# A graph layer on one core: gathered rows split into two float32r halves, h transposed kept in DRAM

## The chip, the cores and the metric

The kernel runs on one core of a Trainium2 chip. The core has five engines that work side by side and meet at semaphores: TensorE (PE, matrix products into PSUM), VectorE (DVE), ScalarE (ACT), GpSimd (POOL) and SyncE (SP). SP, ACT and POOL also issue DMA transfers, which 16 DMA engines of the core carry out between DRAM and the on-chip memory SBUF. The metric is the device time of one execution in microseconds.

## The reference, cut to what matters

```python
h = jnp.maximum(_layernorm(x, axis=-1), 0.0)          # x: 12500 x 256, float32
agg = jax.ops.segment_sum(h[src], dst, num_segments=N)  # 200000 edges, dst sorted
z = (1.0 + eps_gin) * h + agg
t = jnp.dot(z, W1) + b1                                # 256 -> 512
t = jax.nn.relu(_batchnorm(t, g1, bt1))                # statistics over all 12500 rows
conv_out = jnp.dot(t, W2) + b2                         # 512 -> 256
out = x + jax.nn.relu(_batchnorm(conv_out + h, g2, bt2))
```

`src` and `dst` have 200000 entries between 0 and 12499. For each edge the row `src` of h is added into row `dst` of the aggregate. `dst` comes sorted, so neighbouring edges have neighbouring targets. Everything is float32.

## The kernel before, in words

The rows are cut into 25 chunks of 512 (the last has 212). Four stages follow one another, all in `fast()`.

1. **Layernorm** (L274 to L294). A chunk of x is loaded with four consecutive rows in each partition. VectorE takes the statistics, ScalarE applies them with the ReLU (L259). The rows go to a table in DRAM, `h_tab`, from which they are gathered later. TensorE transposes the chunk (L285), and VectorE and ScalarE copy the result into `hT` (L292, L294), which stays in SBUF to the end: 25 tiles, features in partitions, nodes along the columns. Since four rows lie in a partition, the copy has a stride of four.

2. **Gather and first layer** (L297 to L420). The 200000 edges are cut into 1563 tiles of 128 edges (the last has 64), and these into 131 groups of 12 (`GT`). `gather(i)` has POOL issue one indirect DMA a tile (L328): it reads 128 indices from a column of `srcT` in SBUF and brings 128 rows of h, 1 KB each, into a group's buffer `gt`. The pool `gat` has `AHEAD + 1` = 3 such buffers; POOL is two groups ahead. `sums(i)` makes a one-hot matrix `oh` of each edge's target relative to the first target of its group (VectorE, L353) and has TensorE add up the group's rows by target: 12 products of `oh` with `gt` in one PSUM tile `ps` (L362). Products of float32 show as two passes in the trace, so a group has 24. The sums are copied to `zs` (ScalarE, L367); a second one-hot, `at` (VectorE, L369), says at which column of the result they belong. `put(i)` transposes and places them by two products (L380), and VectorE adds the result into the chunk's `zc` (L389), which ScalarE has filled with (1 + eps) h from `hT` (L342). As soon as no later group can reach a chunk, `first_layer` multiplies it by W1 (L397), takes statistics (L401), and stores t in `t_tab` in DRAM. The column numbers that both one-hots are compared with, `col`, are kept in PSUM.

3. **Second layer** (L425 to L446). Each chunk of t is loaded, normalized (ScalarE, L434), multiplied by W2 (L441), added to `hT` (L445), and its statistics are taken.

4. **Output** (L451 to L472). ScalarE normalizes `hT` (L460), TensorE transposes it back (L467), VectorE adds x (L471), and ACT's queue stores the rows.

The order of instructions on each engine comes from a scheduler that follows the program's order and moves instructions where its own estimate of times suggests it. Each engine, and each DMA queue that SP, ACT or POOL feeds, takes its instructions strictly in that order. Dependencies between engines become semaphore waits.

The lines that matter below: L328 (gathers, POOL), L353, L369 and L389 (VectorE in the gather stage), L362 (`ps`, TensorE), L342 and L367 (ScalarE), L285 to L294 (transposes and copies of h), L460 to L472 (output).

Of the kernel before, what the change touches and what calls it, by code (L numbers as in the profile page):

```python
# [7 lines left out]
F32 = mybir.dt.float32  # L8
I32 = mybir.dt.int32
AF = mybir.ActivationFunctionType  # L10
OP = mybir.AluOpType
# [3 lines left out]
P = 128  # L15
R = 4
EPS = 1e-5
GT = 12
MARGIN = 76
AHEAD = 2  # L20

# [7 lines left out]
def kernel(  # L29
# [16 lines left out]
    nc = tc.nc  # L46
    N, D = x.shape
# [214 lines left out]

    def fast():
        with ExitStack() as fs:
            keep = fs.enter_context(tc.tile_pool(name="keep", bufs=1))
            t_tab = dram.tile([NCH, P, HC, CH], F32, name="t_tab")

            hT = [keep.tile([P, DC, w * R], F32, name=f"hT{g}") for g, (_, w) in enumerate(chunks)]


            with tc.tile_pool(name="ln", bufs=3) as ln, tc.tile_pool(
                name="ps_h", bufs=2, space=PSUM
            ) as ps_h:
                for g in range(NCH):  # L274
                    n0, w = chunks[g]
                    n = w * R
                    xt = ln.tile([P, R, D], F32, name="xt", bufs=4)
                    move(nc.sync, xt, x, g, store=False)
                    ht = ln.tile([P, R, D], F32, name="ht")
                    layernorm(ln, xt, w, ht)  # L280
                    move(nc.sync, ht, h_tab, g, store=True)
                    pz = ps_h.tile([P, DC, CH], F32, name="pz")
                    for d in range(DC):
                        for c in range(R):
                            nc.tensor.transpose(  # L285
                                pz[:, d, c * w : (c + 1) * w], ht[:w, c, d * P : (d + 1) * P],
                                ident[:w, :w],
                            )
                        side = hT[g][:, d, :].rearrange("p (w c) -> p c w", c=R)
                        came = pz[:, d, :n].rearrange("p (c w) -> p c w", c=R)  # L290
                        if d % 2:
                            nc.scalar.copy(side, came)  # L292
                        else:
                            nc.vector.tensor_copy(side, came)  # L294


            with ExitStack() as es:  # L297
                gat = es.enter_context(tc.tile_pool(name="gat", bufs=AHEAD + 1))
                sel = es.enter_context(tc.tile_pool(name="sel", bufs=2))
                zcp = es.enter_context(tc.tile_pool(name="zc", bufs=3))  # L300
                tsp = es.enter_context(tc.tile_pool(name="ts", bufs=2))
# [20 lines left out]
                def gather(i):  # L322
                    t0, n = groups[i]
                    gs = []
                    ga = gat.tile([P, GT, D], F32, name="gt")
                    for t in reversed(range(t0, t0 + n)):
                        rows = left if t == full_tiles else P
                        nc.gpsimd.indirect_dma_start(  # L328
                            out=ga[:rows, t - t0, :], out_offset=None, in_=h_tab,
                            in_offset=bass.IndirectOffsetOnAxis(ap=srcT[:rows, t : t + 1], axis=0),  # L330
                        )
                        gs.append((t - t0, rows))
                    gathered[i] = ga, gs

                zc = {}

                def z_chunk(c):
                    if c in zc or c >= NCH:
                        return
                    n = chunks[c][1] * R  # L340
                    zc[c] = zcp.tile([P, DC, CH], F32, name="zc")
                    nc.scalar.activation(zc[c][:, :, :n], hT[c], AF.Copy, scale=gin1)  # L342

                def span(i):
                    return STEP * i - MARGIN, STEP * i - MARGIN + WIDE

                summed = {}

                def sums(i):

                    t0, n = groups[i]
                    oh = sel.tile([P, GT, P], F32, name="oh")
                    nc.vector.tensor_tensor(  # L353
                        oh[:, :n, :],
                        col[:, :P].unsqueeze(1).to_broadcast([P, n, P]),
                        dstT[:, t0 : t0 + n].unsqueeze(2).to_broadcast([P, n, P]),
                        op=OP.is_equal,
                    )
                    ga, gs = gathered.pop(i)
                    ps = ps_s.tile([P, D], F32, name="ps")  # L360
                    for k, (j, rows) in enumerate(gs):
                        nc.tensor.matmul(  # L362
                            ps, lhsT=oh[:rows, j, :], rhs=ga[:rows, j, :], start=(k == 0),
                            stop=(k == n - 1),
                        )
                    zs = sel.tile([P, D], F32, name="zs", bufs=3)
                    nc.scalar.copy(zs, ps)  # L367
                    at = sel.tile([P, WIDE], F32, name="at")
                    nc.vector.tensor_scalar(  # L369
                        at, col, shift[:, i : i + 1], None, op0=OP.is_equal  # L370
                    )
                    summed[i] = zs, at

                def put(i):

                    lo, hi = span(i)
                    zs, at = summed.pop(i)
                    pz = ps_z.tile([P, DC, CH], F32, name="pz2")
                    for d in range(DC):
                        nc.tensor.matmul(  # L380
                            pz[:, d, :WIDE], lhsT=zs[:, d * P : (d + 1) * P], rhs=at, start=True, stop=True
                        )
                    for c in range(max(lo, 0) // CH, -(-min(hi, N) // CH)):
                        z_chunk(c)
                        a, b = max(lo, c * CH, 0), min(hi, (c + 1) * CH, N)
                        if a >= b:
                            continue
                        side = zc[c][:, :, a - c * CH : b - c * CH]
                        nc.vector.tensor_add(side, pz[:, :, a - lo : b - lo], side)  # L389

                def first_layer(c):
# [13 lines left out]

                done = 0
                for i in range(min(AHEAD, NG)):
                    gather(i)
                for i in range(NG + 1):
                    if i + AHEAD < NG:  # L410
                        gather(i + AHEAD)
                    if i < NG:
                        sums(i)
                    if i == 0:
                        continue
                    put(i - 1)
                    nxt = span(i)[0] if i < NG else N
# [5 lines left out]


            with tc.tile_pool(name="tin", bufs=4) as tin, tc.tile_pool(name="tsb", bufs=2) as tsb, tc.tile_pool(  # L425
                name="ps_y", bufs=4, space=PSUM
            ) as ps_y:
                for g in range(NCH):
                    n = chunks[g][1] * R
                    ti = tin.tile([P, HC, CH], F32, name="ti")  # L430
                    nc.sync.dma_start(ti[:, :, :n], t_tab[g, :, :, :n])
                    tT = tsb.tile([P, HC, CH], F32, name="tT")
                    for f in range(HC):
# [4 lines left out]
                    for d in range(DC):  # L438
                        py = ps_y.tile([P, CH], F32, name="py")
                        for f in range(HC):  # L440
# [3 lines left out]
                            )  # L444
                        nc.vector.tensor_add(hT[g][:, d, :], py[:, :n], hT[g][:, d, :])  # L445
                        nc.vector.bn_stats(st2[:, d, g, :], hT[g][:, d, :])  # L446

            sc2, of2 = norm(keep, st2, mv2, DC, g2c, bt2c, b2c, "2")


            with tc.tile_pool(name="xin", bufs=6) as xin, tc.tile_pool(name="ysb", bufs=3) as ysb, tc.tile_pool(  # L451
                name="ps_o", bufs=3, space=PSUM
            ) as ps_o:
                for g in range(NCH):
                    n0, w = chunks[g]
                    xt = xin.tile([P, R, D], F32, name="xr")
                    move(nc.sync, xt, x, g, store=False)
                    yr = ysb.tile([P, DC, R, P], F32, name="yr")
                    for d in range(DC):
                        nc.scalar.activation(  # L460
                            yr[:, d, :, :w], hT[g][:, d, :].rearrange("p (w c) -> p c w", c=R),
                            AF.Relu, bias=of2[:, d : d + 1], scale=sc2[:, d : d + 1],
                        )
                    po = ps_o.tile([P, R, D], F32, name="po")
                    for c in range(R):
                        for d in range(DC):
                            nc.tensor.transpose(  # L467
                                po[:w, c, d * P : (d + 1) * P], yr[:, d, c, :w], ident
                            )
                    ot = ysb.tile([P, R, D], F32, name="ot")  # L470
                    nc.vector.tensor_add(ot[:w], po[:w], xt[:w])  # L471
                    move(nc.scalar, ot, out, g, store=True)  # L472

# [250 lines left out]
```

## Time and profile before

| | us |
|---|---|
| median of 3 runs (lowest, highest) | 2654.84 (2652.75, 2655.27) |
| the profiled execution's own time | 2652.91 |
| its span, first to last instruction | 2651.0 |
| layernorm, up to the start of the first gather | to 149.1 |
| gathers, start of the first to end of the last | 149.1 to 2362.2 |
| second layer, first to last product with W2 | 2392 to 2558.5 |
| output stage | 2558.5 to 2651 |

| from 149 to 2362 us | busy us of 2213 |
|---|---|
| POOL | 1481.5 |
| TensorE, passes | 1314.4 |
| VectorE | 431.2 |
| ScalarE | 123.7 |
| DMA engines (share) | 0.34 |

How to read the lines. A line of the group view names the source line, engine, operation, output and inputs with their shapes, and how many there were; behind the first bar stand the busy time in us and the mean of one in ns; behind the second the idle time of the engine just before these instructions, and what ended it. "issue" is time in which the engine waited for nothing that the profile shows. "remote" is a semaphore whose sender the profile does not show. The view of waits gives engine, line, what was waited for, the total in us, how often, and the longest. In the timeline a line has its start, its duration, and in brackets the idle time before it. PE stands for passes of TensorE, PEld for its weight loads.

### The profile page before, as it was taken

The numbers are of one execution on the slowest core, as the hardware profiler recorded it, in microseconds if no ns is written. First come the engines' busy times: TensorE is split into PE (matmuls) and PEld (weight loads), VectorE is DVE, ScalarE is ACT, GpSimd is POOL, SyncE is SP. The second block draws the span as 40 slices with busy tenths as digits, with TensorE's granted clock in tenths as the row PEclk, the third lists the DMA queues.
The fourth block names the chain that finished last, engine by engine and source line by source line (L and its number), as shares of the span: only waits on it lengthen the run. The fifth ranks groups of instructions, "written<-read, shape, count | busy, mean of one in ns | idle before, by whom it ended". The sixth has DMA issues, their size and how long they took to land.

```text
span 2651.0 us, 14241 instructions
## 1 busy us (share of the span) xinstructions
PE 1623.6 (61%) x4881; PEld 1029.4 (39%) x4881; DVE 633.8 (24%) x1017; ACT 346.8 (13%) x561; POOL 1483.4 (56%) x1575
## 2 busy tenths in 40 slices
PE   3564556755665576556456556666565656569985
PEld 2333344433443343334334334434343334444444
DVE  6611121211221122112112112121121212124443
ACT  4710000000000000000000000000000000004446
POOL 0056667666766666666676676666666676640000
PEclk6566677776776786767777766767776677779985
DMA  5633333333333333333333333333333333325437
GB/s 176 227 101 90 95 101 115 105 95 101 115 105 95 111 105 105 96 111 105 107 97 109 106 98 102 110 105 112 95 105 110 91 114 102 111 78 214 159 130 281
DMA packets 101342, 310.96 MB, mean 117 GB/s; under 512 B 27684, under 2 KB 32362, under 8 KB 95118
## 3 DMA queue, kind: packets, MB, share of 16 engines
q0 software_dynamic: 75008, 204.90, 26.3%
q1 hardware_dynamic: 21744, 91.21, 9.6%
q10 hardware_dynamic: 4510, 13.86, 1.3%
q8 instruction: 41, 0.67, 0.1%
q14 instruction: 39, 0.32, 0.0%
HBM read 258.66 MB, written 51.20 MB: 117 GB/s over the span
## 4 chain that ended last, share of the span: by engine, by line
issue 28%; PE 26%; POOL 25%; another core or an unknown queue 9%; DMA 3%; DVE 2%; ACT 2%; ACTq 0%; POOLq 0%
POOL gt L328 25%; PE ps L362 13%; PE py L441 6%; PE ph L397 4%; DMA gt<-h_tab,srcT 3%; PE pz L380 2%; ACT yr L460 2%; DVE oh L353 1%; PE po L467 1%; DVE zc L389 1%; DVE ot L471 0%; DVE mv L229 0%; DVE at L369 0%; DVE st L401 0%
## 5 line engine op out<-in xcount | busy, mean ns | idle before, releaser
L328 POOL DMA_INDIRECT gt<-h_tab,srcT x1563 | 1481.8, 948 | 850.5 <-issue 458.2
L362 PE MATMUL ps<-gt,oh 128*128 128x256 f32 x3126 | 987.1, 447 | 643.0 <-issue 559.4
L362 PEld LDWEIGHTS ps<-gt,oh 128*128 128x128 f32 x3126 | 672.5, 221 | 949.5 <-issue 738.8
L389 DVE TENSOR_TENSOR zc<-pz,zc 128x560 f32<-128x560 f32 (+9 forms) x203 | 101.0, 527 | 1518.0 <-PE ps L362 863.5
L380 PE MATMUL pz<-at,zs 128*128 128x280 f32 x524 | 194.5, 498 | 181.4 <-DVE zc L389 114.8
L367 ACT COPY zs<-ps 128x256 f32<-128x256 f32 x131 | 48.9, 373 | 1739.4 <-PE ps L362 1147.3
L397 PE MATMUL ph<-zc,w1s 128*128 128x512 f32 (+1 forms) x400 | 197.0, 648 | 80.4 <-DVE zc L389 56.9
L353 DVE TENSOR_TENSOR oh<-col,dstT 128x1536 f32<-128x1536 f32 x131 | 227.8, 1739 | 14.5 <-issue 14.5
L380 PEld LDWEIGHTS pz<-at,zs 128*128 128x128 f32 x524 | 119.5, 237 | 235.0 <-issue 209.2
L441 PE MATMUL py<-tT,w2s 128*128 128x512 f32 (+1 forms) x400 | 169.5, 587 | 4.6 <-ACT tT L434 4.6
L397 PEld LDWEIGHTS ph<-zc,w1s 128*128 128x128 f32 x400 | 82.4, 211 | 181.1 <-issue 117.5
L401 DVE BATCH_NORM_STATS2 st<-ph 128x6 f32<-128x512 f32 (+1 forms) x100 | 68.4, 684 | 265.9 <-remote 93.7
L441 PEld LDWEIGHTS py<-tT,w2s 128*128 128x128 f32 x400 | 76.4, 192 | 97.7 <-issue 86.7
L402 ACT COPY ts<-ph 128x512 f32<-128x512 f32 (+1 forms) x100 | 57.3, 573 | 334.0 <-DVE st L401 251.9
L285 PE MATMUL pz<-ident,ht 128*128 128x128 f32 (+1 forms) x200 | 65.0, 442 | 54.1 <-ACT ht L259 19.5
L434 ACT ACTIVATE tT<-ti,of,sc 128x512 f32<-128x512 f32 (+1 forms) x100 | 72.3, 796 | 91.3 <-issue 86.4
L467 PE MATMUL po<-ident,yr 128*128 128x128 f32 (+1 forms) x200 | 47.6, 413 | 35.6 <-ACT yr L460 35.6
L285 PEld LDWEIGHTS pz<-ident,ht 128*128 128x128 f32 (+1 forms) x200 | 36.6, 205 | 82.5 <-ACT ht L259 40.7
L369 DVE TENSOR_SCALAR at<-col,shift 128x280 f32<-128x280 f32 x131 | 65.5, 500 | 0.0
L460 ACT ACTIVATE yr<-hT,of,sc 128x512 f32<-128x512 f32 (+1 forms) x50 | 59.9, 1276 | 20.1 <-DVE ot L471 19.2
L445 DVE TENSOR_TENSOR hT<-py,hT 128x512 f32<-128x512 f32 (+1 forms) x50 | 33.9, 678 | 100.9 <-PE py L441 100.9
L467 PEld LDWEIGHTS po<-ident,yr 128*128 128x128 f32 (+1 forms) x200 | 37.5, 214 | 45.7 <-ACT yr L460 45.7
(68 smaller groups left out, 307.6 us busy)
## 6 DMA issues: line engine op xcount, KB each, us to landing
gt<-h_tab,srcT POOLq DMA_INDIRECT x1563
t_tab<-ts SPq DMA_DIRECT2D x24, 1024.0 KB
ti<-t_tab SPq DMA_DIRECT2D x24, 1024.0 KB
xt<-in_x_dram SPq DMA_DIRECT2D x24, 512.0 KB
h_tab<-ht SPq DMA_DIRECT2D x24, 512.0 KB
xr<-in_x_dram SPq DMA_DIRECT2D x24, 512.0 KB
out_dram<-ot ACTq DMA_DIRECT2D x24, 512.0 KB
rawi_d<-in_dst_dram SPq DMA_DIRECT2D x1, 768.0 KB
```

The lines of the kernel that those rows point to most:

```text
L285: nc.tensor.transpose(pz[:, d, c * w : (c + 1) * w], ht[:w, c, d * P : (d + 1) * P], ident[:w, :w],)
L328: nc.gpsimd.indirect_dma_start(out=ga[:rows, t - t0, :], out_offset=None, in_=h_tab, in_offset=bass.IndirectOffsetOnAxis(ap=srcT[:rows, t ...
L353: nc.vector.tensor_tensor(oh[:, :n, :], col[:, :P].unsqueeze(1).to_broadcast([P, n, P]), dstT[:, t0 : t0 + n].unsqueeze(2).to_broadcast([P ...
L362: nc.tensor.matmul(ps, lhsT=oh[:rows, j, :], rhs=ga[:rows, j, :], start=(k == 0), stop=(k == n - 1),)
L380: nc.tensor.matmul(pz[:, d, :WIDE], lhsT=zs[:, d * P : (d + 1) * P], rhs=at, start=True, stop=True)
L389: nc.vector.tensor_add(side, pz[:, :, a - lo : b - lo], side)
L397: nc.tensor.matmul(ph[:, :n], lhsT=w1s[:, d, f * P : (f + 1) * P], rhs=zc[c][:, d, :n], start=(d == 0), stop=(d == DC - 1),)
L401: nc.vector.bn_stats(st1[:, f, c, :], ph[:, :n])
L434: nc.scalar.activation(tT[:, f, :n], ti[:, f, :n], AF.Relu, bias=of1[:, f : f + 1], scale=sc1[:, f : f + 1],)
L441: nc.tensor.matmul(py[:, :n], lhsT=w2s[:, f, d * P : (d + 1) * P], rhs=tT[:, f, :n], start=(f == 0), stop=(f == HC - 1),)
L460: nc.scalar.activation(yr[:, d, :, :w], hT[g][:, d, :].rearrange("p (w c) -> p c w", c=R), AF.Relu, bias=of2[:, d : d + 1], scale=sc2[:, d ...
L467: nc.tensor.transpose(po[:w, c, d * P : (d + 1) * P], yr[:, d, c, :w], ident)
```

## The change

Five things change together.

1. **The split.** After a group has been gathered, ScalarE copies its rows into a tile of type float32r (a shorter mantissa, `hi`), and VectorE subtracts that from the rows (`lo`, also float32r). The two halves of a row lie side by side, 512 columns, and one product a tile takes both. The two sums are added when they leave PSUM: ScalarE copies the second, VectorE adds the first.
2. **Six groups of rows in SBUF**: `AHEAD` goes from 2 to 5, and the pool of `gt` buffers with it from three to six. Gathers of a group are issued in ascending order instead of descending.
3. **h transposed in DRAM.** `hT` is gone. Each transposed chunk is stored in `h_cols`; `z_chunk` loads it a chunk ahead of use, and the second layer loads it again into `yT`.
4. **Slots.** A chunk has row c * 128 + p in slot c of partition p, not row 4 p + c. A partition's piece of x, `h_tab` or the output is therefore 1 KB instead of 4 KB, and transposed columns come in the nodes' order without a stride. One statistics instruction takes two slots, interleaved, and the two sums that it forms for even and odd places are the two rows' own.
5. **Order.** In the loop over groups, joining and placing the sums of the group before now stand ahead of the split of this one, and the add into `zc` behind its products.

```diff
-AHEAD = 2
+AHEAD = 5
...
                     st = ln.tile([P, R, 3], F32, name="st")
+                    for c in range(0, slots, 2):
+                        nc.vector.bn_stats(
+                            st[:, c : c + 2, :].rearrange("p c s -> p (c s)"),
+                            xt[:, c : c + 2, :].rearrange("p c d -> p d c"),
+                        )
...
-                        side = hT[g][:, d, :].rearrange("p (w c) -> p c w", c=R)
-                        came = pz[:, d, :n].rearrange("p (c w) -> p c w", c=R)
                         if d % 2:
-                            nc.scalar.copy(side, came)
+                            nc.scalar.copy(hc[:, d, :n], pz[:, :n])
                         else:
-                            nc.vector.tensor_copy(side, came)
+                            nc.vector.tensor_copy(hc[:, d, :n], pz[:, :n])
+                    nc.sync.dma_start(h_cols[g, :, :, :n], hc[:, :, :n])
...
-                    for t in reversed(range(t0, t0 + n)):
+                    for t in range(t0, t0 + n):
...
-                    nc.scalar.activation(zc[c][:, :, :n], hT[c], AF.Copy, scale=gin1)
+                    nc.sync.dma_start(zc[c][:, :, :n], h_cols[c, :, :, :n])
+                    nc.scalar.activation(zc[c][:, :, :n], zc[c][:, :, :n], AF.Copy, scale=gin1)
...
+                def split(i):
...
+                    hl = sel.tile([P, GT, 2, D], F32R, name="hl")
+                    whole = min(n, max(0, full_tiles - t0))
+                    for j0, j1, rows in ((0, whole, P), (whole, n, left)):
+                        if j0 == j1:
+                            continue
+                        hi, lo = hl[:rows, j0:j1, 0, :], hl[:rows, j0:j1, 1, :]
+                        nc.scalar.copy(hi, ga[:rows, j0:j1, :])
+                        nc.vector.tensor_tensor(lo, ga[:rows, j0:j1, :], hi.bitcast(F32), op=OP.subtract)
+                    chosen[i] = oh, hl
+
+                def sums(i):
...
-                    ps = ps_s.tile([P, D], F32, name="ps")
-                    for k, (j, rows) in enumerate(gs):
+                    ps = ps_s.tile([P, 2, D], F32, name="ps")
+                    for j in range(n):
+                        rows = left if t0 + j == full_tiles else P
                         nc.tensor.matmul(
-                            ps, lhsT=oh[:rows, j, :], rhs=ga[:rows, j, :], start=(k == 0),
-                            stop=(k == n - 1),
-                        )
+                            ps, lhsT=oh[:rows, j, :], rhs=hl[:rows, j, :, :], start=(j == 0), stop=(j == n - 1)
+                        )
+                    summed[i] = ps
+
+                def join(i):
+                    ps = summed.pop(i)
                     zs = sel.tile([P, D], F32, name="zs", bufs=3)
-                    nc.scalar.copy(zs, ps)
+                    nc.scalar.copy(zs, ps[:, 1, :])
+                    nc.vector.tensor_add(zs, ps[:, 0, :], zs)
...
                     if i + AHEAD < NG:
                         gather(i + AHEAD)
+                    pz = None
+                    if i > 0:
+                        join(i - 1)
+                        pz = put(i - 1)
                     if i < NG:
+                        split(i)
                         sums(i)
...
-                    put(i - 1)
+                    add(i - 1, pz)
...
                     nc.sync.dma_start(ti[:, :, :n], t_tab[g, :, :, :n])
+                    nc.sync.dma_start(yT[g], h_cols[g, :, :, :n])
...
-                            yr[:, d, :, :w], hT[g][:, d, :].rearrange("p (w c) -> p c w", c=R),
-                            AF.Relu, bias=of2[:, d : d + 1], scale=sc2[:, d : d + 1],
+                            yr[:, d, :n], yT[g][:, d, :], AF.Relu, bias=of2[:, d : d + 1], scale=sc2[:, d : d + 1]
```

## The prediction

> **What bounds the kernel now.** I read three views in turn. First the page: the busy shares and the costliest groups of instructions.
>
> ```profile
> span 2651.0 us, 14241 instructions
> ...
> PE 1623.6 (61%) x4881; PEld 1029.4 (39%) x4881; DVE 633.8 (24%) x1017; ACT 346.8 (13%) x561; POOL 1483.4 (56%) x1575
> ...
> L328 POOL DMA_INDIRECT gt<-h_tab,srcT x1563 | 1481.8, 948 | 850.5 <-issue 458.2
> L362 PE MATMUL ps<-gt,oh 128*128 128x256 f32 x3126 | 987.1, 447 | 643.0 <-issue 559.4
> ```
>
> No engine is full, PE is only the busiest on average. POOL's line is one gather of 128 rows, 1563 times, from 149.1 us (start of the first) to 2362.2 us (end of the last): 2213 of the 2651 us are the gather stage. Its 948 ns plus the usual gap of about 0.30 us (458.2 us in 1501 times) make a gather every 1.25 us, so POOL alone would need 1563 x 1.2515 = 1956 us. The view of waits says what the other 255 us are.
>
> ```profile
> PEld ps L362 <- issue: 738.8, 520, 5.4
> PE ps L362 <- issue: 559.4, 363, 3.1
> ...
> POOL gt L328 <- issue: 458.2, 1501, 0.6
> ...
> POOL gt L328 <- PE ps L362: 194.0, 42, 9.6
> ...
> POOL gt L328 <- remote: 78.7, 17, 6.6
> ```
>
> The last two lines are 59 waits, 272.7 us, for a gather buffer; less the 59 gaps of 0.3 us that would have been there anyway, 255 us. So POOL sets the time, and every ninth part of it is lost to a full ring of three groups. The timeline of one such wait shows why PE was late.
>
> ```profile
> 1007.11 0.59 PE L362 MATMUL ps<-gt,oh 128*128 128x256 f32 x1 [2.22 <-issue]
> ...
> 1008.51 0.28 PEld L362 LDWEIGHTS ps<-gt,oh 128*128 128x128 f32 x1 [2.52 <-issue]
> ...
> 1010.20 0.94 POOL L328 DMA_INDIRECT gt<-h_tab,srcT  x1 [0.30 <-issue]
> ...
> 1014.81 3.32 PE L362 MATMUL ps<-gt,oh 128*128 128x256 f32 x5 [1.52 <-issue]
> ...
> 1017.26 0.94 POOL L328 DMA_INDIRECT gt<-h_tab,srcT  x1 [6.11 <-PE ps L362]
> ```
>
> PE issues one instruction (a weight load or a pass) every 1.4 us, though the rows landed long before; a few us after POOL has run dry it goes on at full rate. In the stretches that I followed this begins after PE has caught up with the gathers and waits for each one. The trace doesn't say what throttles the issue.
>
> **The change part by part.** One group is 12 gathers, 12 x 1.25 = 15.0 us of POOL; 130 full groups and one of 3.
>
> PE (L362): two passes of 256 columns a tile become one of 512. A 512-column pass takes 434 ns in the second layer (L441: 166.6 us for 384), so 12 x 0.43 = 5.2 us a group; between half of that and double (10.4, if the type still takes two passes) it stays under 15.0. PE isn't the bound, so this saves nothing by itself. But a matmul now waits for VectorE's split of a whole group instead of for each gather, and the ring holds six groups. Of the 255 us between nothing and all is regained; I take all, because both the state that precedes the slow issue (waiting for single gathers) and the short ring go. If slow issue stays, a ring twice as long has a stall about half as often: 127 us remain.
>
> ACT adds the rounded half, 12 x 256 = 3072 elements: 1.15 us for 1024 (zc, L342) and 0.82 ns for each more (0.583 against 0.373 us for 512 and 256, ts and zs), so 2.8 us a group. VectorE adds the subtraction: two-input operations in SBUF take 1.786 us for 1562 elements and 0.295 for 131 (L195), so 0.295 + 2941 x 1.042 ns = 3.36 us, beside one-hot 1.75, 0.5, 0.74 and the new add of 0.33 (256 elements): 6.7 of 15.0 us. Both engines lie under POOL. The path from subtraction to the next one (first two matmuls, join, placing, add into zc) is some 7 us, also under 15.0; behind a late subtraction are the group's matmuls and, six groups on, the buffer. Nothing of this is on the path, unless it disturbs POOL.
>
> That is the point where a rule is weighed against the rows. The row is this answer of the trace on L328:
>
> ```profile
> L328 POOL DMA_INDIRECT gt<-h_tab,srcT x1563: 902/949/1102, 149.1 to 2361.3; - x196
> ```
>
> Minimum, median and maximum: no gather takes over 1.1 us, though VectorE is busy for 431 us in this stage. But all its operations there (oh, at, zc, the statistics) read at most one operand from SBUF: `col` is kept in PSUM, the others read matmul results. The new subtraction reads both of its operands from SBUF, which no operation does while gathers run. The Trainium skill, page "SBUF — State Buffer", section "Who interferes with whom": "A DVE instruction with two SBUF inputs contends with a GpSimd instruction that reads SBUF, not with one that only writes it", and the one that comes second blocks until the first is through. A gather reads its 128 indices from srcT in SBUF. The same section infers that generating descriptors needs the write side alone, which would leave gathers free; it doesn't speak of indices. So the cost of a subtraction lies between 0 (by the row) and 3.36 us a group (by the rule, if it starts just as a gather would). If it blocks, it starts on average half a gather's pitch before the next index read: 3.36 - 0.63 = 2.73 us a group, 131 x 2.73 = 358 us. I take the rule, as the row covers no such operation: by the row alone the sum would be 2399 us, by the rule 2757.
>
> Layernorm stage, from 29.3 us to the first gather at 149.1. ACT's copy into hT shrinks from 1.06 to about 0.58 us (ts, a plain copy of 512 from PSUM), VectorE's too, and four statistics of 0.40 and four aggregates of 0.17 become two of about 0.70 (L401, 512 elements): ACT goes from 3.7 to 3.2 us a chunk, VectorE from 4.0 to 2.5. Against this the transposed h is written to DRAM: 25 more stores on SP's queue, 12.8 MB beside 25.6. From 30 to 148 us the DMA engines are busy 0.61 at 218 GB/s, so 357 GB/s at full; 38.4 MB are 108 us at the least, without bubbles and with rows of 1 KB moved as efficiently as the 4 KB runs before. And SP's order, as the built program has it, changes: x loads no longer alternate with stores but come four or five at a time, behind the store of the transposed chunk before them, so that each batch of five begins with a load of 2 MB (5.9 us) that little covers. Five batches, half of it hidden: 15 us. Stage between 112 and 160 us; I take 137, 17 more.
>
> Elsewhere: zc comes by a 512 KB load a chunk ahead of use, on SP behind the t_tab store, with some 85 us of gathers as cover; ACT scales it in place for the same 1.15 us. Without that cover it would be about 4 us a chunk. The last group's tail (29.8 us from the last gather to the second layer) loses PE's slow stretch and gains split and join: 27. Second layer: PE-bound for 166.5 us at full clock; yT adds 0.5 MB per 6.6 us, 0.22 of the DMA engines beside 0.42: hidden. Output stage, 92.5 us: ACT is busy 60.2 of it, with yr at 1.30 us for 512 strided elements; unstrided as tT it takes 0.81, 24 us less over 50. The DMA engines are at 0.73, 68 us at full, so at most 24 go, and none if 1 KB rows cost more: I take 11.
>
> Sum against the profiled execution, 2652.9 us (span 2651.0 and 1.9 around it; the runs' median is 2654.8, 0.07% above): first gather at 149.1 + 17 = 166; gathers 1956 + 358 = 2314; tail 27; second layer 166.5; output 81.5; 1.9 around: **2757 us**.
>
> **The rivals.** (1) The subtraction doesn't touch the gathers, and PE keeps up: 2757 - 358 = 2399. For it: the flat durations on L328 and the page's own inference. Against: the rule's words fit, and `col` in PSUM is never a second SBUF operand. It decides from 1.95 us a group on: (2653 - 2399) / 131; below that delay the kernel is faster, above it slower. (2) As (1), but PE's slow issue stays, with half the stalls: 2399 + 127 = 2526. For it: its cause isn't known, and PE will still idle some 10 us a group while gathers run. (3) A partial block, 0.3 to 1.9 us a group, if an index read only loses to a subtraction now and then: 2440 to 2650. That the pass count isn't halved would change nothing, since 10.4 us fit.
>
> **How the numbers follow.** Block: 0.54, and its own range is 2690 to 2815 (2.4 to 3.0 us a group, layernorm stage 115 to 155). Rival 1: 0.28. Rival 2: 0.12. Rival 3: 0.06, of which about 0.02 within 0.2% (what a measurement of this kernel can tell from no change). Faster 0.28 + 0.12 + 0.03 = 0.43, same 0.02, slower 0.55. The range must hold both sides: from 2388, which leaves out the better end of rival 1 (about 0.1), to 2808, which leaves out full blocking together with a slow layernorm stage (0.08).
>
> **What the profile will show.** Right: gathers whose duration, or the gap before them, reaches 3 to 4 us, once a group and beside the subtraction; their mean pitch near 1.48 us; no waits of POOL for PE. Rival 1 has a pitch of 1.25 us throughout and POOL busy without a break. Rival 2 has waits of 5 to 7 us for VectorE, every sixth group, with PE at one instruction per 1.4 us before them. The first gather should start at 160 to 175 us, ps should have 1563 matmuls of 512 columns, and the output stage should end with DMA as its limit. What would make the forecast wrong above all is index reads that don't pass the port in question.

## The result, and the profile after

The changed kernel takes 2747.37 us (median of 4 runs, 2746.06 to 2749.40) against 2654.04 us of the kernel before beside it (2652.75 to 2655.27): a ratio of 1.035 with a 95% interval of 1.033 to 1.037. It is slower, and 10 us under the predicted 2757.

The page of the changed kernel, with the lines that answer to those shown of before:

```profile
span 2747.6 us, 12311 instructions
...
PE 1212.0 (44%) x3310; PEld 765.9 (28%) x3310; DVE 1090.4 (40%) x1130; ACT 655.9 (24%) x691; POOL 1831.3 (67%) x1576
...
L372 POOL DMA_INDIRECT gt<-h_tab,srcT x1563 | 1828.7, 1170 | 498.1 <-issue 474.3
L422 PE MATMUL ps<-hl,oh 128*128 128x512 f32 x1563 | 569.4, 512 | 887.2 <-DVE hl L412 871.4
L412 DVE TENSOR_TENSOR hl<-gt,hl 128x3072 fp32r<-128x3072 f32 x132 | 437.5, 3314 | 965.3 <-ACT hl L411 520.7
L411 ACT CAST hl<-gt 128x3072 fp32r<-128x3072 f32 x132 | 358.7, 2718 | 1670.5 <-DMA gt<-h_tab,srcT 1666.0
```

PE's busy time fell from 1623.6 to 1212.0 us, since one pass of 512 columns stands for two of 256. POOL's rose from 1483.4 to 1831.3 us with the same 1563 gathers: the mean of one went from 948 to 1170 ns. The view of the gathers' line says that it isn't all of them that got longer:

```profile
L372 POOL DMA_INDIRECT gt<-h_tab,srcT x1563: 902/949/4078, 164.0 to 2467.9; - x196
```

Minimum and median are those of before (902 and 949 ns), the maximum is 4078 ns where it was 1102. Counted from the trace, 129 gathers take over 1.2 us, 3.63 us on average, and the rest take what they took. The view of waits has one line left for POOL in this stage that matters, and its longest entry is 0.3 us: POOL never waits for a buffer, where before it did so 59 times.

```profile
POOL gt L372 <- issue: 474.3, 1556, 0.3
```

The timeline shows two of the long gathers (start, duration, engine; only POOL and VectorE's subtraction are copied):

```profile
1005.88 0.94 POOL L372 DMA_INDIRECT gt<-h_tab,srcT  x1 [0.30 <-issue]
...
1006.42 3.35 DVE L412 TENSOR_TENSOR hl<-gt,hl 128x3072 fp32r<-128x3072 f32 x1
...
1007.13 3.46 POOL L372 DMA_INDIRECT gt<-h_tab,srcT  x1 [0.30 <-issue]
1010.89 0.95 POOL L372 DMA_INDIRECT gt<-h_tab,srcT  x1 [0.30 <-issue]
...
1017.82 3.36 DVE L412 TENSOR_TENSOR hl<-gt,hl 128x3072 fp32r<-128x3072 f32 x1 [3.02 <-DMA gt<-h_tab,srcT]
...
1018.41 3.59 POOL L372 DMA_INDIRECT gt<-h_tab,srcT  x1 [0.30 <-issue]
```

The gather that is under way when the subtraction starts (1005.88) keeps its 0.94 us. The next one, begun inside the subtraction, ends 0.82 us after the subtraction's end: 1006.42 + 3.35 = 1009.77, and 1007.13 + 3.46 = 1010.59. The same holds at 1018.41 (21.18 and 22.00), and for all 129 long gathers the distance is 0.82 to 0.83 us. The last column has 0.30 before each: the hold-up is inside the gather, not ahead of it.

The stages, from the first and last instructions of their lines; here the second layer reaches to the end of its last product, 3 us further than in the table of before. The two columns on the right are the same two kernels on another chip, which the first experiment is about.

| us | before | after | before, other chip | after, other chip |
|---|---|---|---|---|
| to the first gather | 149.1 | 164.0 | 149.9 | 165.5 |
| gathers | 2213.2 | 2304.8 | 1953.1 | 2302.8 |
| to the first product with W2 | 29.7 | 30.3 | 19.9 | 30.5 |
| products with W2, to the end of the last | 169.5 | 169.6 | 169.5 | 169.6 |
| output | 89.5 | 78.8 | 90.0 | 79.1 |
| span | 2651.0 | 2747.6 | 2382.4 | 2747.5 |

For the stages besides, the view of stretches (length, busy time of PE, its weight loads, VectorE, ScalarE and POOL, granted clock, share of the DMA engines, GB/s), for the layernorm, gather and output stages of after:

```profile
30.00:163.00 133.00, 52.87 (x196) 28.83 (x196) 57.50 (x132) 74.55 (x153) 1.40 (x3) 1.00 0.88 305
164.00:2469.00 2305.00, 922.96 (x2428) 606.60 (x2428) 899.42 (x805) 464.98 (x371) 1828.66 (x1563) 0.70 0.34 104
2669.00:2747.60 78.60, 39.64 (x196) 35.65 (x196) 32.60 (x36) 36.10 (x51) 0.00 (x0) 0.73 0.88 300
```

The first and the last are now set by DMA (0.88; before 0.61 and 0.73), the gather stage by POOL.

### The profile page after: what moved, and what is told of

The parts are those of the page before. It is cut to its first block, busy times and chain, and to the rows that moved or that the text cites. A ratio compares the mean times of both kernels' runs of the same rounds, so it can differ in the third digit from the quotient of the medians.

```text
span 2747.6 us, 12311 instructions
## 1 busy us (share of the span) xinstructions
PE 1212.0 (44%) x3310; PEld 765.9 (28%) x3310; DVE 1090.4 (40%) x1130; ACT 655.9 (24%) x691; POOL 1831.3 (67%) x1576
## 4 chain that ended last, share of the span: by engine, by line
POOL 62%; issue 21%; PE 9%; DMA 4%; DVE 2%; ACT 1%; SPq 0%; ACTq 0%; POOLq 0%; DVEq 0%
POOL gt L372 62%; PE py L518 6%; DMA out_dram<-ot 1%; DMA xt<-in_x_dram 1%; PE pz L332 1%; DMA gt<-h_tab,srcT 1%; PE ph L465 1%; ACT ht L324 1%; PE po L543 0%; DVE ot L549 0%; DVE hl L412 0%; ACT hc L336 0%; DVE st L310 0%; DVE hc L338 0%; SPq L287 0%
## 5 line engine op out<-in xcount | busy, mean ns | idle before, releaser
L372 POOL DMA_INDIRECT gt<-h_tab,srcT x1563 | 1828.7, 1170 | 498.1 <-issue 474.3
L422 PE MATMUL ps<-hl,oh 128*128 128x512 f32 x1563 | 569.4, 512 | 887.2 <-DVE hl L412 871.4
L412 DVE TENSOR_TENSOR hl<-gt,hl 128x3072 fp32r<-128x3072 f32 x132 | 437.5, 3314 | 965.3 <-ACT hl L411 520.7
L411 ACT CAST hl<-gt 128x3072 fp32r<-128x3072 f32 x132 | 358.7, 2718 | 1670.5 <-DMA gt<-h_tab,srcT 1666.0
L422 PEld LDWEIGHTS ps<-hl,oh 128*128 128x128 f32 x1563 | 374.6, 247 | 1027.0 <-issue 901.7
L443 PE MATMUL pz<-at,zs 128*128 128x280 f32 x524 | 251.6, 629 | 24.6 <-DVE zs L431 22.9
L398 DVE TENSOR_TENSOR oh<-col,dstT 128x1536 fp32r<-128x1536 f32 x131 | 227.7, 1738 | 0.0
L443 PEld LDWEIGHTS pz<-at,zs 128*128 128x128 f32 x524 | 159.5, 309 | 104.5 <-DVE zs L431 31.9
L518 PE MATMUL py<-tT,w2s 128*128 128x512 f32 (+1 forms) x400 | 169.6, 587 | 4.6 <-ACT tT L511 4.6
L332 PE MATMUL pz<-ident,ht 128*128 128x128 f32 x196 | 52.9, 446 | 77.6 <-ACT ht L324 63.8
L431 DVE TENSOR_TENSOR zs<-ps,zs 128x256 f32<-128x256 f32 x131 | 54.6, 417 | 35.4 <-issue 28.9
```

The costliest lines, as they stand in the source:

```text
L332: nc.tensor.transpose(pz[:, c * P : (c + 1) * P], ht[:, c, d * P : (d + 1) * P], ident)
L372: nc.gpsimd.indirect_dma_start(out=ga[:rows, t - t0, :], out_offset=None, in_=h_tab, in_offset=bass.IndirectOffsetOnAxis(ap=srcT[:rows, t ...
L398: nc.vector.tensor_tensor(oh[:, :n, :], col[:, :P].unsqueeze(1).to_broadcast([P, n, P]), dstT[:, t0 : t0 + n].unsqueeze(2).to_broadcast([P ...
L411: nc.scalar.copy(hi, ga[:rows, j0:j1, :])
L412: nc.vector.tensor_tensor(lo, ga[:rows, j0:j1, :], hi.bitcast(F32), op=OP.subtract)
L422: nc.tensor.matmul(ps, lhsT=oh[:rows, j, :], rhs=hl[:rows, j, :, :], start=(j == 0), stop=(j == n - 1))
```

## The experiments

Times of one experiment are compared with the kernel before on the same chip, because the chips turned out to differ.

**The two kernels again, on another chip.** No edit.

> The kernel before, unchanged, with a profile on the chip of these runs, where its time was 2387 us and not 2654. Theory (POOL's 255 us of waits come from PE's slow issue, and this chip doesn't show it): gathers every 1.25 us from first to last, no wait for a buffer, no stretch with one PE instruction in 1.4 us, 2387 us; PE still waits for each single gather, so waiting alone doesn't cause slow issue. Rival (the clock of POOL or memory is faster here): a pitch under 1.25 us.

> The kernel after, unchanged, on the chip of these runs. Theory (its time is POOL's 1956 us, 346 us of blocked gathers, and the stages around them, none of which depends on PE's slow issue): 2747 us whichever chip, so 15% over a before of 2387 us. Rival (it profits from this chip as the kernel before does): 2480 to 2500 us, 3.5 to 4.5% over.

Measured: the kernel before 2390.66 us (18 runs; the same kernel as the comparison beside it, 24 runs, 2391.97), the changed kernel 2748.39 us (2746.48 to 2750.46), a ratio of 1.149 (1.147 to 1.151). The changed kernel takes the same time on both chips, the kernel before is 263 us quicker on this one. Its gather line and its waits there:

```profile
L328 POOL DMA_INDIRECT gt<-h_tab,srcT x1563: 903/946/1098, 149.9 to 2102.1; - x196
```

```profile
PEld ps L362 <- DMA gt<-h_tab,srcT: 904.2, 1016, 3.0
POOL gt L328 <- issue: 459.6, 1509, 0.3
...
PE ps L362 <- DMA gt<-h_tab,srcT: 399.5, 678, 2.6
```

POOL runs through without a pause of over 1 us, and its stage takes 1953.1 us, the 1956 us that the prediction worked out for POOL alone. So the 255 us of buffer waits are no trait of the kernel: they are there on some chips and not on others. And PE waits for single gathers here in 1016 and 678 places, without falling into the slow issue of one instruction per 1.4 us: in the gather stage, 393 of its instructions start 1.35 to 1.45 us after the one before in the first trace of this kernel, and one here. That waiting for single gathers brings it on, as the prediction supposed, doesn't hold.

**One operand of the subtraction from PSUM.** The changed kernel, with the same instruction on VectorE in length and number, but only one operand in SBUF.

```diff
-                        nc.vector.tensor_tensor(lo, ga[:rows, j0:j1, :], hi.bitcast(F32), op=OP.subtract)
+                        other = col[:rows, :D].unsqueeze(1).to_broadcast([rows, j1 - j0, D])
+                        nc.vector.tensor_tensor(lo, ga[:rows, j0:j1, :], other, op=OP.subtract)
```

> The kernel after, but the subtraction takes its second operand from PSUM (the column numbers) and not from the rounded half in SBUF; length, output and place stay. It leaves out the true low half: what is summed there is the row less the column number. Theory (a second operand in SBUF blocks the gathers' read of their indices): no gather over 1.1 us, the 346 us of long gathers go, 2747 - 346 = 2401 us. Rival (any long VectorE operation over the gathered rows, or its writing, blocks them): 129 long gathers as before, 2747 us.

Measured: 2393.15 us (one run; before 2387.14 on this chip). The timeline, where a gather begins inside the operation:

```profile
1005.18 0.95 POOL L372 DMA_INDIRECT gt<-h_tab,srcT  x1 [0.30 <-issue]
1005.52 3.35 DVE L413 TENSOR_TENSOR hl<-gt,col 128x3072 fp32r<-128x3072 f32 x1 [7.38 <-DMA gt<-h_tab,srcT]
1006.43 0.95 POOL L372 DMA_INDIRECT gt<-h_tab,srcT  x1 [0.30 <-issue]
1007.68 0.95 POOL L372 DMA_INDIRECT gt<-h_tab,srcT  x1 [0.30 <-issue]
```

VectorE is busy for the same 3.35 us and writes the same tile, and no gather is longer than 1.12 us. The gather stage takes 1953.6 us where the changed kernel has 2302.8 to 2304.8. All 130 of these operations have gathers that begin inside them, and none is held up. The whole block hangs on the second SBUF operand.

**Such an operation added to the kernel before, and its like on ScalarE.** Each group's rows are replaced by themselves, once by VectorE with two SBUF operands, once by a copy on ScalarE of nearly the same length.

```diff
                     ga, gs = gathered.pop(i)
...
+                            rs = ga[:rows, j0:j1, :]
+                            nc.vector.tensor_tensor(rs, rs, rs, op=OP.max)
```

```diff
+                            rs = ga[:rows, j0:j1, :]
+                            nc.scalar.copy(rs, rs)
```

> The kernel before, with one VectorE operation a group that takes the larger of the gathered rows and themselves, in place: two operands in SBUF, 3072 elements, values unchanged. PE then waits for it instead of for each gather; the ring stays at three. Theory (it blocks gathers as the subtraction does, and PE's slow issue needs waiting for single gathers): 2653 - 255 + 346 = 2744 us, long gathers once a group, no waits for a buffer. If the ring of three is what made the stalls, up to 255 of them stay: up to 2999. If only the float32r halves or the new order cost time: 2398 to 2653.

> The kernel before, with ScalarE copying each group's gathered rows onto themselves (2.7 us a group, values unchanged) between gathers and products. PE waits for it instead of for each gather; ring of three, float32 products in two passes, everything else as before. Theory (PE's slow issue, and with it POOL's 255 us of waits, needs PE to wait for single gathers): 2653 - 255 = 2398 us. Rival (the ring of three is too short, or two passes too slow): 2653 us or little less, with waits of 5 to 7 us left.

Measured: with VectorE 2714.19 us (one run), with ScalarE 2398.59 us (2397.67 to 2399.48), a ratio of 1.005 (1.003 to 1.007); before 2387.14. In the first, 130 gathers are long, in the second none:

```profile
1006.00 3.36 DVE L364 TENSOR_TENSOR gt<-gt 128x3072 f32<-128x3072 f32 x1 [8.31 <-DMA gt<-h_tab,srcT]
1006.72 3.46 POOL L328 DMA_INDIRECT gt<-h_tab,srcT  x1 [0.30 <-issue]
```

```profile
1008.74 2.75 ACT L364 COPY gt<-gt 128x3072 f32<-128x3072 f32 x1 [12.20 <-DMA gt<-h_tab,srcT]
1009.37 0.95 POOL L328 DMA_INDIRECT gt<-h_tab,srcT  x1 [0.30 <-issue]
```

So one such operation by itself carries the block over into the kernel before: 317.0 us more in its long gathers, and a stage of 2274.3 us where it has 1953.1 without. The 30 us less than expected are the place where it starts: a gather begins 0.79 us (median) after the operation here and 0.55 us in the changed kernel, so less of the operation is left, 3.36 + 0.82 - 0.79 = 3.39 us for a gather against 3.63, which are the measured means of both. The copy was also to show whether PE's slow issue goes when it waits once a group. On this chip the kernel before has no slow issue, so it tells nothing of that.

**Twelve short subtractions for the long one.** The work is that of the changed kernel.

```diff
-                        nc.vector.tensor_tensor(lo, ga[:rows, j0:j1, :], hi.bitcast(F32), op=OP.subtract)
+                        for j in range(j0, j1):
+                            nc.vector.tensor_tensor(
+                                hl[:rows, j, 1, :], ga[:rows, j, :], hl[:rows, j, 0, :].bitcast(F32), op=OP.subtract
+                            )
```

> The kernel after, with the subtraction of a group cut into one of 256 elements a tile: 12 of 0.43 us in place of one of 3.36. Theory with the port released after every instruction: a gather's index read meets an operation of 0.43 us in a third of the cases and then waits 0.2 us, and about four gathers fall beside the twelve: 0.3 to 0.9 us a group, 2401 + 40 to 120 = 2440 to 2520 us. Theory with the port held while VectorE has the next one ready: 12 x 0.43 - 0.6 = 4.5 us a group, 2401 + 590 = 2990 us. If the length of the operation doesn't matter: 2747.

> The changed kernel with twelve subtractions of one tile for the one of twelve, again. Theory that the long subtraction alone holds the gather up: 2464 us on a chip without pauses, as measured before. On a chip where the kernel before pauses (2655 us) it tells whether the split products, with a wait once a group and six groups of buffers, keep clear of the pauses: 2464 if so, a ratio of .928; 2464 plus 100 to 255, 2560 to 2720, if the pauses are of the chip and the buffers can't cover them.

Measured: 2463.63 us (2456.13 to 2468.92), a ratio of 1.032 (1.030 to 1.035) to 2387.14; a second time, on another chip without pauses, 2463.03 us (2461.79 to 2468.37), 1.032 (1.031 to 1.034). In the timeline of the first:

```profile
1005.28 4.11 DVE L413 TENSOR_TENSOR hl<-gt,hl 128x256 fp32r<-128x256 f32 x12
...
1006.12 1.06 POOL L372 DMA_INDIRECT gt<-h_tab,srcT  x1 [0.30 <-issue]
1007.49 1.04 POOL L372 DMA_INDIRECT gt<-h_tab,srcT  x1 [0.30 <-DVE hl L413]
1008.83 1.04 POOL L372 DMA_INDIRECT gt<-h_tab,srcT  x1 [0.30 <-issue]
1010.17 0.95 POOL L372 DMA_INDIRECT gt<-h_tab,srcT  x1 [0.30 <-issue]
```

VectorE works without a pause for 4.11 us, with two SBUF operands, and yet a gather beside it usually loses only 0.1 us: it ends 0.82 us after the end of one short operation, as if it had waited for that one alone. The stage shrinks from 2304.8 to 2019.0 us (2019.7 the second time). It isn't free: 13 gathers in the first run and 12 in the second still took 1.2 to 4.3 us, 27 us in all each time; eight in each run were held up to the end of the last of a row, and took 4.03 to 4.29 us. Why these few, the traces don't say. A chip with pauses it didn't meet, so what it would make of them stays open.

**The split alone taken out.** The changed kernel with its six buffers, h in DRAM, slots and order, but float32 products straight from the gathered rows.

```diff
-                    oh = sel.tile([P, GT, P], F32R, name="oh")
+                    oh = sel.tile([P, GT, P], F32, name="oh")
...
+                    hl = ga
...
-                    nc.scalar.copy(zs, ps[:, 1, :])
-                    nc.vector.tensor_add(zs, ps[:, 0, :], zs)
+                    nc.scalar.copy(zs, ps)
```

> The kernel after without the split: products take the gathered rows as float32 in two passes, without ScalarE's copy, VectorE's subtraction and the add of two sums; ring of six, h transposed in DRAM, new slots and order stay. Theory (only the subtraction costs): 2747 - 346 = 2401 us on any chip without slow issue; with it, stalls of half the 255 us, 2526. Rival (other parts of the change cost too, by more than the layernorm stage's 15 us): over 2420 on a chip where the kernel before takes 2387.

Measured: 2399.33 us (2394.48 to 2401.79), beside 2391.97 of before and 2748.39 of the changed kernel on this chip: the split costs 349 us, and its long gathers there have 349.1 us over their usual length. The other four parts together are 1.0035 (1.0021 to 1.0049) of the kernel before.

**Three buffers in place of six.** In the changed kernel, `AHEAD` back to 2.

> The kernel after with a ring of three groups in place of six. Theory (a buffer is free some 7 us after its rows landed, and the ring is never full): 2747 us, no waits of POOL for a buffer. Rival (the long ring hides the latency of split and products): waits for VectorE's subtraction, some us a group, up to 2747 + 130 x 3 = 3140 us.

Measured: 2758.24 us (2757.63 to 2758.85), 10 us more than with six. The gather stage is 2304.9 us, with 129 long gathers and no buffer wait worth naming: on this chip the longer ring does nothing for the gathers. Most of the 10 us (8.6) are lost between the last gather and the second layer (39.1 us in place of 30.5), by the order on SP's queue:

```profile
2491.59 1.29 SPq L508 DMA_DIRECT2D yT<-h_cols  x3
...
2497.80 1.95 SPq L508 DMA_DIRECT2D yT<-h_cols  x2
...
2501.26 9.79 SPq L507 DMA_DIRECT2D ti<-t_tab  x5
2507.79 4.33 ACT L511 ACTIVATE tT<-ti,of,sc 128x512 f32<-128x512 f32 x6 [9.79 <-DMA ti<-t_tab]
```

Five loads of the transposed h, needed only after the first products, stand ahead of the first chunk of t, for which ScalarE waits 9.79 us. In the changed kernel that chunk's load is issued first, at 2490.92 us. The scheduler set the order anew when the buffers changed.

**Only the slots, the paired statistics and the order.** h transposed stays in SBUF as before, three groups of rows, float32 products (the gathers keep their ascending order, too).

```diff
-AHEAD = 5
+AHEAD = 2
...
-            h_cols = dram.tile([NCH, P, DC, CH], F32, name="h_cols")
+            hT = [keep.tile([P, DC, w * R], F32, name=f"hT{g}") for g, (_, w) in enumerate(chunks)]
...
-                    nc.sync.dma_start(h_cols[g, :, :, :n], hc[:, :, :n])
...
-                    nc.sync.dma_start(zc[c][:, :, :n], h_cols[c, :, :, :n])
-                    nc.scalar.activation(zc[c][:, :, :n], zc[c][:, :, :n], AF.Copy, scale=gin1)
+                    nc.scalar.activation(zc[c][:, :, :n], hT[c], AF.Copy, scale=gin1)
```

> Of the change only the new slots, the paired statistics and the order of the loop: h transposed stays in SBUF, ring of three, float32 products of the gathered rows, no split. Theory (the slots help where ScalarE's and VectorE's strided copies were the limit, the stores of transposed h are what made the layernorm stage longer): first gather at 125 to 140 us against 150, output stage some 10 us shorter, gathers 1953 us: 2387 - 10 to 25 - 10 = 2352 to 2367 us where the kernel before takes 2387 to 2392. Rival (rows of 1 KB cost the DMA engines what the copies save): 2380 to 2390. On a chip where the kernel before takes 2654 us, its stalls should stay: 2620 to 2635.

> The new slot order and paired statistics, with h transposed in SBUF, three groups and float32 products straight from the gathered rows, a second time on whatever chip it meets. If its gain of 34 us on a chip where the kernel before has pauses of PE is the earlier start of the gathers (122 in place of 149 us) and the shorter output, and not something of that chip, it stays where the pauses are missing: 2387 less 27 of the start less some 10 to 19 of the output is 2340 to 2350 us, a ratio of .980 to .985. With pauses it repeats 2621, ratio .988.

Measured on a chip with pauses: 2621.21 us (2616.57 to 2626.55) against 2655.03, a ratio of 0.988 (0.986 to 0.989); on one without: 2347.25 us (2346.56 to 2348.93) against 2387.17, 0.983 (0.982 to 0.985). This version beats both kernels on both kinds of chip. In the second run its span is 37.8 us shorter than that of the kernel before on the other chip without pauses: 26.9 by an earlier first gather (123.0 against 149.9), 12.0 in the output stage (78.0 against 90.0), 0.5 before the second layer, less 1.6 in the gathers and the second layer. Its layernorm stage, in the view of stretches:

```profile
30.00:122.00 92.00, 52.91 (x196) 28.85 (x196) 57.26 (x129) 72.89 (x152) 1.40 (x3) 0.50 0.89 279
```

The DMA engines are as full (0.89) as in the changed kernel, but have only x and `h_tab` to move. That puts a price on storing h transposed: 164.0 - 123.0 = 41 us later for the first gather. Measured by whole kernels it is 52 us (2399.33 against 2347.25, six buffers and a longer tail of 25.8 us against 19.4 in it), on two chips whose kernel before differs by 5.

**A wait once a group, on a chip with pauses.** The version just shown, with ScalarE copying each group's rows onto themselves before PE reads them.

```diff
                     hl = ga
+                            nc.scalar.copy(ga[:rows, j0:j1, :], ga[:rows, j0:j1, :])
```

> As the slots alone, with ScalarE copying each gathered group onto itself before the products, so that PE waits once a group. Theory: no effect where PE shows no slow issue but 8 to 12 us at the end of the gathers (copy and twelve products follow the last rows of a group): 2362 to 2378 us. On a chip where the kernel before takes 2654 us, PE no longer waits for single gathers and the 255 us of stalls go: 2362 to 2378 us there too. Rival for that chip (slow issue comes whenever PE idles beside gathers, whatever it waits for): 2620 to 2640 us.

Measured: 2652.55 us (2649.18 to 2661.57), 0.999 (0.998 to 1.000) of the kernel before and 31 us more than without the copy. 71 pauses of POOL of over 1 us come to 294 us beyond the usual gap of 0.3 (without the copy, 69 and 261 us). Two lines of its waits, and one pause in the timeline:

```profile
DVE oh L396 <- remote: 1096.8, 68, 47.0
ACT zs L425 <- remote: 698.1, 51, 16.5
```

```profile
1084.19 4.48 PE L417 MATMUL ps<-gt,oh 128*128 128x256 f32 x20
...
1094.65 2.07 PE L417 MATMUL ps<-gt,oh 128*128 128x256 f32 x4 [5.98 <-issue]
...
1103.99 0.94 POOL L371 DMA_INDIRECT gt<-h_tab,srcT  x1 [0.30 <-issue]
1106.79 1.76 DVE L396 TENSOR_TENSOR oh<-col,dstT 128x1536 f32<-128x1536 f32 x1 [21.18 <-remote]
1106.85 0.37 ACT L425 COPY zs<-ps 128x256 f32<-128x256 f32 x1 [12.25 <-remote]
1107.49 0.94 POOL L371 DMA_INDIRECT gt<-h_tab,srcT  x1 [2.56 <-ACT zs L425]
```

The group's last four products end at 1096.7 us, but ScalarE copies their sums only at 1106.85, 10.1 us later, when POOL has run dry (its last gather ended at 1104.93). So pauses come with a single wait a group too: with the first experiment, waiting for single gathers is neither enough for them nor needed. Slow issue isn't needed either. Steps of 1.35 to 1.45 us between PE's instructions number only 5 in the version without the copy and 3 here.

## Why the prediction was right

**The block.** 131 x 2.73 = 358 us were predicted, 129 x 2.69 = 346.5 us came, and the second, third and fourth experiments show that it is the second SBUF operand: without it 0, with it in the other kernel 317, with the operation cut into twelve some 65. Taking the rule of the Trainium skill, page "SBUF — State Buffer", section "Who interferes with whom", over the flat row of before was the choice that decided. The same section's inference that generating descriptors needs the write side alone, which stood behind rival 1, doesn't carry over to these gathers: 129 were held up. That the read of their indices is the reason would fit, but no run here isolates it. The term was right for a cruder reason than the true one, though. The prediction took the subtraction's start as random within a gather's pitch. It is bound to it: the landing of the group's last rows starts the split, and the next gather follows 0.55 us (median; 0.39 to 0.70 in eight of ten) after the subtraction. The delay is the rest of the subtraction and the 0.82 us that a gather still needs, less its usual 0.95: 3.36 - 0.55 + 0.82 - 0.95 = 2.68.

**The 255 us.** As predicted, they are gone (no pause over 1 us). The reason given for it is the step that failed. "Waiting for single gathers" isn't what brings on slow issue, since the kernel before does it on another chip without any (1016 and 678 waits, no pause). And the pauses need neither: the version with the copy has 294 us of them with one wait a group and hardly any slow issue. The longer ring wasn't shown to do it either: the run with three buffers was on a chip where nothing pauses. That the term came out right was, as far as these runs show, luck. What keeps the changed kernel clear of the pauses on its first chip (half the instructions on PE, the ring, or the 17.6 us that a group now takes in place of 15.0) is open.

**The base.** It follows that the prediction's break-even of 1.95 us a group holds only where the kernel before pauses. On the other chips, rival 1 would have been no gain at all: without a block the parts measured 2393 and 2399 us against 2387 and 2392.

**The small terms.** The first gather was to come at 166 and came at 164.0. The 137 us assumed for that stage were a choice inside a range, not a sum. The net was right, the parts weren't seen: the slots and statistics bring it forward by 27 us, the stores of h transposed push it back by 41. The tail was to take 27 and took 30.3: it lost PE's slow stretch (the kernel before takes 19.9 us on the chip without it) and gained as much again, which is put down to the split, the join and the loads without a test. The output stage was to gain 11 and gained 10.7, with DMA as its limit, as foretold. A pass of 512 columns took 512 ns on average where 434 was assumed, 6.1 us a group, under 15.0 and so without effect; the split took 2.75 and 3.36 us where 2.8 and 3.36 were worked out. Against the profiled execution's own time, 2749.4, the forecast was 7.6 us high: 9.2 in the gather stage (2304.8 against 2314) and 2.0 ahead of it, less 3.3 in the tail and 0.4 behind it.

## What to carry to other kernels

While GpSimd issues indirect gathers, keep VectorE's long operations to one operand in SBUF: put the other in PSUM, give the work to ScalarE (a copy of 2.75 us there held up none), or cut it into short instructions, since a gather then usually waits for one of them only (eight of 1563 still waited for a whole row). A wait that the profile can't explain on the engine that shows it ("issue", "remote") may be a trait of the chip on which it was taken, or of the recording there; a change that is to remove it needs a base on a second chip. And a change of five parts can hide a good one: here two of them were worth 34 to 40 us and were buried under 349.

## What the runs showed of the hardware

**Two kinds of chip.** The kernel before took 2387 to 2392 us on three of the chips, and 2654 to 2655 us in the first runs and on one chip met later (whether that is the first chip again isn't known), its single runs on one chip within 0.5%. Of the 269 us between the two spans, 260 are in the gather stage, in pauses of POOL for PE's results, and 10 in the tail behind it. The traces give two hints. On the chips with pauses the engines that wait for PE are put down to "remote" or go on late, and in the trace's record of semaphore updates those of PE come 2.1 to 3.5 us apart in the stretch shown above (1086 to 1107 us), long after the products. And the record has holes there. Of PE's updates in the kernel before, 2186 are recorded on the chip without pauses and 1905 on that with them; of those by which the gathers land, 25008 and 3845. So PE's idle time under "issue" can hide waits for landings. The changed kernel has 13830 of its 25008 recorded on the first chip, and no pause. Updates delivered late while gathers run would fit, and so would a chip on which the recording itself holds the engines up. Every run here was recorded, so neither is shown, and why chips differ isn't known.

**Where a gather can be held up.** A gather already under way when the operation began was never held up: 127 of the changed kernel's subtractions started inside one, at 0.25 us or later from its start, and in the run with three buffers one started at 0.16 us. The next gather always was, and ended 0.82 us after the operation. So of its 0.95 us, about the first 0.13 can be held up (0.95 less 0.82, an estimate). The read of the indices would fall within them, which no run here isolates.
